# q, k and v of groups 1 to 14 as 49 products of 128 cubed, and a running count that places the other work around them

## The chip, the cores and the metric

One core of a Trainium2 chip runs the kernel. The metric is device time in microseconds (us), the median of several executions. The engines named below: TensorE (PE in the profile; its weight loads are the row PEld), VectorE (DVE), ScalarE (ACT), GpSimd (POOL), and the DMA queues that SyncE (SP) and GpSimd issue into. SBUF is the on-chip memory, PSUM the eight accumulation banks that TensorE writes.

## The reference

x holds 128 graphs of 64 nodes with 512 features, all in float32. Four layers follow one another, each of the form x = layernorm(x + f(x)):

```
layer 0:  y = relu(S (x W1) + b1), layernorm, S (y W2) + b2, plus x      (512 -> 1024 -> 512)
layer 1:  attention-like weights from y = x @ w, then A @ x @ w
layer 2:  x = relu(adj (x W1) + b1); x = relu(adj (x W2) + b2); adj (x W3) + b3
layer 3:  qkv = x @ Wqkv; 8 heads of 64; softmax over 64 nodes, mixed with adj and exp(-adj); times v; @ W_out + b_out
```

So each group of nodes passes through eleven products with 512x512 weights (W2 counts double), and between them small 64x64 products for each graph.

## The kernel before

**Tiling.** A group is 8 graphs, 512 rows, so there are 16 groups (NGRP) and every large product is 512x512x512. `multiply` (from L539 in the profile's rows on, through `product`) does it by Winograd's form of Strassen's scheme: four quadrants of 256, seven products of 256 cubed instead of eight. The seven are named B11, T1, T2, B21, T3, B22, T4. The left side's sums are made on DVE by `Left.sums` (L518 to L521), the sums on the weight's side are made once, by `Weight.making`, and kept in DRAM; `Weight.load` (L236, L238) brings one 256x256 tile for each product into a ring of RING = 20 tiles. `Stream.pump` issues these loads on SP's queue as ring slots come free. In a product, `ten.matmul` at L539 runs four times, each with a moving operand of 256 columns.

The results are joined as they come: the accumulators a and c are used again, their intermediate values go out by `snap` (u1, u5, u2: L555, on ACT, or on DVE where a residual or bias is added), and DVE adds the quadrants (L568 for the first, in bank b, which is "c_" in the names; L589; L598); the last is a copy on ACT (L608) or an add (L610).

**Stages.** Group q runs through `first_half` (a: layers 0 and 1) and `second_half` (b: layers 2 and 3); a step of the main loop works at the same time on group s in a, s-1 in b and s-2 in the tail t of `second_half` (the end of attention, Wout, the last layer norm). The lists `start`, `order`, `step_1`, `step_last` name the pieces in order, such as "b.q1", "b.k", "a.w1a"; a piece is what a generator does up to its next `yield`. Group 0 has its own path `first_group`, and group 15 ends in `last_rows`.

**Order.** Inside this, the framework's scheduler decides where an instruction goes on its engine, unless the code holds it: `in_turn` puts an instruction after the newest one of an engine, `behind(key)` after a recorded one, and engines in `strict` keep the order of the text. Each engine works through its own queue in order.

**Around the change.** In layer 3, `second_half` transposes x (L1186) into the left side xT, runs q, k, then `scores` (L1356, L1367), v, `softmax` (L1334 to L1342), `turn_probs` (L1391, L1398), `attend` (L1415), `taken` (L1430) and Wout. The tail's last `layer_norm` (bn_stats L457, sqrt L447, scaling L463) and its store stand between b.q and b.k. The scaling of layer 1's norm is split by `late`. bo is added to x by one DVE instruction (L1201), gb3 by four (L749, in `shifted`). `load` brings a group's x on SP's queue (`load_group`). Pools: ps_acc with 4 PSUM banks for the large products, pv and sps, ps_gt with 4 for the small ones; big with 8 tiles of 8 KB a partition.

Of the kernel before, what the change touches and what calls it, by code (L numbers as in the profile page):

```python
# [14 lines left out]
P = 128  # L15
C = 64
# [21 lines left out]
RING = 20  # L38
# [3 lines left out]
def kernel(  # L42
# [37 lines left out]
    big = ctx.enter_context(tc.tile_pool(name="big", bufs=8))  # L80
    sp = ctx.enter_context(tc.tile_pool(name="sp", bufs=3))
    work = ctx.enter_context(tc.tile_pool(name="work", bufs=7))
# [3 lines left out]
    ps_acc = ctx.enter_context(tc.tile_pool(name="ps_acc", bufs=4, space=bass.MemoryType.PSUM))  # L86
# [8 lines left out]
    nc.vector.memset(eps_t, EPS)  # L95

# [33 lines left out]

    ten, vec, act = Engine(nc.tensor, PE), Engine(nc.vector, DVE), Engine(nc.scalar, ACT)

    def load_group(q):
# [11 lines left out]
        else:  # L145
# [7 lines left out]
            nc.sync.dma_start(out=xg, in_=xsrc)  # L153
# [66 lines left out]
    class Weight:  # L220
        def __init__(self, src, col0, name, halves=1, scaled=False):
            self.src, self.col0, self.name, self.halves, self.scaled = src, col0, name, halves, scaled
            self.kept = []
# [5 lines left out]
        def tile(self, what, q, u):  # L229
            return wring.tile([P, 2, Q], FP, name=f"{self.name}{what}_{q}_{u}", tag="wq")  # L230

# [24 lines left out]
        def making(self, quads):  # L256
# [21 lines left out]
            with in_turn(POOL):  # L278
                for k, t in to_keep:
                    nc.gpsimd.dma_start(out=k, in_=t)  # L280
            yield got
# [46 lines left out]
    w_q, w_k, w_v = (Weight(Wqkv, n * D, f"w{'qkv'[n]}") for n in range(3))  # L328
# [5 lines left out]
    class Stream:  # L334


        def __init__(self, uses):
            self.todo = []
            for wt, q in uses:
                if q == 0:  # L340
# [10 lines left out]
        def pump(self, uses=None):  # L351
            end = len(self.todo) - uses if uses else 0
            while len(self.todo) > end and self.held + self.todo[0][3] <= RING:
                wt, q, what, n = self.todo.pop(0)
                self.held += n
                if what is None and q > 0:
# [42 lines left out]

        def done(self, wt, q, what):  # L400

            if q > 0:
                self.held -= wt.halves
            else:

                self.held -= 2 if what == ORDER[0] else 1
            self.pump()
# [43 lines left out]
    def layer_norm(xg, key, pairs=range(G), late=()):  # L451
# [7 lines left out]
        rs = rstd(mv, G, key, slice(pairs[0], pairs[-1] + 1))  # L459
# [7 lines left out]
        scale(p for p in pairs if p not in late)  # L467
        return lambda: scale(late)

# [34 lines left out]
    class Left:  # L504
# [9 lines left out]
        def sums(self):  # L514
# [3 lines left out]
            vec.tensor_add(s1, s3, self.quad(1, 1))  # L518
            vec.tensor_sub(s2, s1, self.quad(0, 0))
            vec.tensor_sub(s3, self.quad(0, 0), s3)  # L520
            vec.tensor_sub(s4, self.quad(0, 1), s2)  # L521
# [3 lines left out]
            }  # L525
            return self

    def product(acc, lefts, wt_q, what, first, last, flipped):
        ws = stream.take(*wt_q, what)
        n_k = 2 * len(lefts)  # L530
        for blk in range(2):
# [12 lines left out]
        stream.done(*wt_q, what)  # L544

    def multiply(lefts, wt_q, dst, key, flipped=False, res=None, stops=(3,), then=None, held={}, early=False):
# [6 lines left out]
        def snap(ps, m, n, what):  # L553
            t = work.tile([P, 2, Q], FP, name=f"{what}_{key}", tag="w")
# [5 lines left out]
        s1 = snap(pa, 0, 0, "u1")  # L560
# [3 lines left out]
        def first_quadrant():  # L564
            pb = ps_acc.tile([P, 2, Q], FP, name=f"c_{key}", tag="acc")
            product(pb, lefts, wt_q, B21, True, True, flipped)
            with behind(held.get(4)):
                vec.tensor_add(dst(0, 0), pb, s1)  # L568
            if then:
                then(0, 0, dst(0, 0))  # L570
# [17 lines left out]
        product(pa, lefts, wt_q, T3, False, False, flipped)  # L588
        last_add[f"{key}.d"] = vec.tensor_add(dst(1, 1), pa, s5).ins  # L589
# [6 lines left out]
        last_add[f"{key}.p6"] = newest(PE)  # L596
        with behind(held.get(6)):
# [9 lines left out]
        elif res is None:  # L607
            act.copy(dst(1, 0), pa)  # L608
        else:
            vec.tensor_add(dst(1, 0), pa, res(1, 0))  # L610
# [27 lines left out]
    def prepare(g):  # L638
# [49 lines left out]
        if q > 1:  # L688

            s_ps = [ps_acc.tile([P, G, C], FP, name=f"sps_{q}", tag="acc")] * 2  # L690
# [53 lines left out]

    def shifted(g, key):

        with behind(key):
            for p in range(G):
                vec.tensor_add(g["x"][:, p, :], g["x"][:, p, :], gb3_bc)  # L749
# [3 lines left out]
    def first_half(g):  # L753
# [6 lines left out]
        left.sums()  # L760
        yield "c1"
        h = [big.tile([P, 2, DH], FP, name=f"h_{q}_{m}", tag="big") for m in range(2)]
        for n in range(2):
# [8 lines left out]
            yield "w1" + "ab"[n]  # L772

# [837 lines left out]
```

## Time and profile before

| what | value |
|---|---|
| median of 3 runs | 2734.02 us (2733.93 to 2734.05) |
| the profiled execution, span | 2732.1 us |
| granted TensorE clock, mean | 1.000 |
| one group in the steady part (the same product of wo, 867.57 to 1035.54 us) | 167.97 us |
| DVE busy in it | 128.73 us |
| ACT busy in it | 49.36 us |
| DMA moved | 405.14 MB, 148 GB/s on average |
| a store of x, a load of x, a weight tile, from issue to landing | 5.2, 5.8, mostly 2.7 to 3.1 us |

The profiled execution is one run under the profiler; its span goes from the first to the last instruction, and the runs' median is 1.9 us longer. In a row of the groups, the columns are line, engine, operation, output<-inputs, shape and count; then the busy time, the mean of one in ns, and the idle time of the engine just before, with what ended it. In the order of time, a row begins with its start and its length, and merges equal neighbours. A row's length contains its tail, which overlaps with the next instruction: two DVE adds of 0.69 us follow each other at 0.60.

### The profile page before, as it was taken

The page shows a single profiled execution, that of the slowest core. Times are in us where ns is not written, and L with a number is a line of the kernel's source. Part 1 is how long each engine was busy: PE and PEld are TensorE (multiplying, and loading weights), DVE is VectorE, ACT ScalarE, POOL GpSimd, SP SyncE. Part 2 cuts the span into 40 slices and gives each one's busy share as a digit, 9 for nine tenths or more (in the row PEclk, how much of TensorE's full clock was granted, in tenths as well). Part 3 has the DMA queues.
Part 4 walks back from the last instruction along what each step waited for, and adds up shares of the span by engine and source line. Part 5 has one row for each costly group of instructions (what it writes and reads, how often), then busy time and mean ns, then how long its engine had stood idle before and what let it go on. Part 6 is the DMA issues. An engine that isn't in the chain of part 4 may idle for free.

```text
span 2732.1 us, 67726 instructions
## 1 busy us (share of the span) xinstructions
PE 2714.7 (99%) x28770; PEld 2347.7 (86%) x28770; DVE 2077.8 (76%) x4111; ACT 803.9 (29%) x1440; POOL 38.0 (1%) x71
## 2 busy tenths in 40 slices
PE   9999999999999999999999999999999999999998
PEld 7888888888888888888888888888888888888887
DVE  6878687876877778777786877778677687776766
ACT  3323223232232332323223233232322323233232
POOL 2000000000000000000000000000000000000000
PEclk9999999999999999999999999999999999999999
DMA  7545454454544545455454554545545455454541
GB/s 257 179 129 154 123 175 140 142 162 131 173 131 139 168 129 170 130 145 168 134 165 129 146 165 133 164 129 151 163 130 167 130 154 157 128 166 129 158 125 63
DMA packets 309532, 405.14 MB, mean 148 GB/s; under 512 B 57424, under 2 KB 185456, under 8 KB 309232
## 3 DMA queue, kind: packets, MB, share of 16 engines
q1 hardware_dynamic: 304256, 385.45, 48.2%
q0 software_dynamic: 4832, 15.24, 1.5%
q8 instruction: 228, 3.74, 0.6%
q14 instruction: 72, 0.59, 0.1%
q10 hardware_dynamic: 144, 0.13, 0.0%
HBM read 369.78 MB, written 30.93 MB: 147 GB/s over the span
## 4 chain that ended last, share of the span: by engine, by line
PE 96%; DVE 3%; ACT 1%; issue 0%; DMA 0%; DVEq 0%
PE a_l0w L539 15%; PE b_l0w L539 7%; PE a_l2b L539 4%; PE a_q L539 4%; PE a_k L539 4%; PE a_l2a L539 4%; PE a_v L539 4%; PE c_l0w L539 4%; PE a_l1w L539 4%; PE a_wo L539 4%; PE a_l2c L539 4%; PE gt_l L481 3%; PE gt_l0h L481 2%; PE b_l2a L539 2%; PE b_l1w L539 2%; PE b_l2b L539 2%
## 5 line engine op out<-in xcount | busy, mean ns | idle before, releaser
L539 PE MATMUL a_l0w<-w2w,aT_l0h 128*128 128x256 f32 x720 | 164.3, 381 | 0.0
L457 DVE BATCH_NORM_STATS2 st_l<-x 128x6 f32<-128x512 f32 x244 | 157.9, 676 | 0.6
L539 PEld LDWEIGHTS a_l0w<-w2w,aT_l0h 128*128 128x128 f32 x720 | 135.6, 190 | 18.8
L463 DVE TENSOR_SCALAR x<-x,mv_l,rs_l 128x512 f32<-128x512 f32 x244 | 119.3, 543 | 2.2
L539 PE MATMUL b_l0w<-w2w,s_l0h 128*128 128x256 f32 x480 | 108.5, 379 | 0.0
L783 ACT ACTIVATE h<-h 128x1024 f32<-128x1024 f32 (+1 forms) x58 | 55.0, 948 | 178.5 <-DVE h L598 157.4
L539 PEld LDWEIGHTS b_l0w<-w2w,s_l0h 128*128 128x128 f32 x480 | 91.1, 190 | 12.5
L1140 ACT ACTIVATE aT_h<-gth,gb_col 128x256 f32<-128x256 f32 x124 | 47.2, 491 | 159.0 <-PE gth L1128 159.0
L447 ACT ACTIVATE rs_l<-mv_l,eps_t 128x4 f32<-128x4 f32 (+1 forms) x63 | 18.8, 298 | 252.3 <-DVE mv_l L458 245.0
L492 ACT COPY aT_l<-gt_l 128x512 f32<-128x512 f32 x148 | 78.1, 597 | 46.4 <-PE gt_l L481 46.4
L555 DVE TENSOR_TENSOR u_l0w<-a_l0w,b_bc 128x512 f32<-128x512 f32 x56 | 38.6, 689 | 69.2 <-PE a_l0w L539 69.2
L539 PE MATMUL a_l2b<-gwbw,aT_h 128*128 128x256 f32 x360 | 86.6, 383 | 0.0
L539 PE MATMUL a_l2c<-gwcw,aT_h 128*128 128x256 f32 x360 | 86.3, 382 | 0.0
L539 PE MATMUL a_q<-aT_xT,wqw 128*128 128x256 f32 x360 | 85.1, 379 | 0.5 <-ACT aT_xT L1194 0.5
L539 PE MATMUL a_l1w<-ww,aT_l 128*128 128x256 f32 x360 | 85.1, 379 | 0.2 <-ACT aT_l L492 0.2
L539 PE MATMUL a_l2a<-aT_l,gwaw 128*128 128x256 f32 x360 | 85.0, 379 | 0.0
L539 PE MATMUL a_k<-aT_xT,wkw 128*128 128x256 f32 x360 | 85.0, 379 | 0.0
L539 PE MATMUL a_v<-wvw,aT_xT 128*128 128x256 f32 x336 | 81.1, 384 | 0.5 <-issue 0.5
L539 PE MATMUL a_l0w<-w1aw,aT_l 128*128 128x256 f32 x336 | 80.8, 383 | 0.0
L539 PE MATMUL a_wo<-wow,aT_oT 128*128 128x256 f32 x336 | 79.5, 379 | 0.0
L539 PE MATMUL a_l0w<-w1bw,aT_l 128*128 128x256 f32 x336 | 79.4, 379 | 0.0
L539 PEld LDWEIGHTS a_l2c<-gwcw,aT_h 128*128 128x128 f32 x360 | 67.2, 190 | 11.6 <-ACT u_l2c L555 3.0
(532 smaller groups left out, 6489.0 us busy)
## 6 DMA issues: line engine op xcount, KB each, us to landing
w2w<-w2k SPq DMA_DIRECT2D x210, 256.0 KB, 2.7
x<-in_x_dram SPq DMA_DIRECT2D x15, 1024.0 KB, 5.8
w1aw<-w1ak SPq DMA_DIRECT2D x60, 256.0 KB, 2.7
w1bw<-w1bk SPq DMA_DIRECT2D x60, 256.0 KB, 2.8
ww<-wk SPq DMA_DIRECT2D x60, 256.0 KB, 2.7
gwaw<-gwak SPq DMA_DIRECT2D x60, 256.0 KB, 3.4
gwbw<-gwbk SPq DMA_DIRECT2D x60, 256.0 KB, 2.7
gwcw<-gwck SPq DMA_DIRECT2D x60, 256.0 KB, 2.7
```

The lines of the kernel that those rows point to most:

```text
L447: act.activation(rs[:, at], mv[:, at, 1], AF.Sqrt, bias=eps_t)
L457: vec.bn_stats(st, xg[:, p, :])
L463: vec.tensor_scalar(xg[:, p, :], xg[:, p, :], mv[:, p, 0:1], rs[:, p : p + 1], ALU.subtract, ALU.mult)
L481: ten.matmul(ps[g][f * C : (f + 1) * C, c, p, :], src(2 * duo + p)[rows, c0 : c0 + C], mat[rows, 2 * duo + p, :], start=True, stop=True,)
L492: act.copy(o[:, :, :, g, :], ps[g])
L539: ten.matmul(acc[:, blk, :], lhsT, rhs, start=(first and blk == 0 and i == 0), stop=(last and i == n_k - 1), skip_group_check=True,)
L555: last_add[f"{key}.{what}"] = (act.copy(t, ps) if res is None else vec.tensor_add(t, ps, res(m, n))).ins
L783: act.activation(hn, hn, AF.Relu)
L1140: act.activation(o[:, :, h, :], cols, AF.Relu, bias=gb2_col[:, k : k + 1])
```

## The change

- q, k and v of groups 1 to 14 take Strassen's step twice. The class `Deep` lays the seven operands of the outer step in two halves of four and three (DEEP), makes the inner sums on DVE (`more_sums`), and `deep_multiply` runs the inner step's seven stages on both halves, for three weights one after the other and interleaved (`deep_stages`): 49 matmuls of 128x128x128 a weight. Stages end in copies on ACT or adds on DVE; `cross` and `outer_sums` join them. Groups 0 and 15 keep `multiply`.
- The weights' sums of the second step are made on POOL once (`make_deep`) and kept in DRAM; `load_deep` loads four or three 128x128 blocks in one DMA.
- From q to the end of the second W1 block (a.w1b), PE, DVE and ACT keep the order of the text, and an object `side` keeps a count of each engine's time. Other work (the layer 1 output and norm, the layer 3 norm, sums of left sides, relu and stats of h, doubling of x, softmax) is handed to it as generators that name the engine and the duration of each instruction, and it puts one where by its count the engine would else be idle.
- In every `multiply`, u1 is written into a PSUM bank of its own (ps_sum), on which B21 accumulates; the first quadrant is then copied by ACT. A first matmul "full" writes that bank once. ps_acc has 3 banks, and pv and sps use ps_gt.
- Layer norms of layers 1 and 3 scale on ACT (`norm_steps`); softmax takes the maximum negated, and eight exponentials of 64 columns on ACT with bias and sum.
- gb3 (groups 1 to 14) and bo are added to x by an accumulating DMA of POOL (`add_rows`), bo's behind a small copy that waits for the first result of `turn_probs`.
- x of groups 2 and up is loaded on POOL's queue after k (loadx), not with the rest of its group. RING is 16, big has 9 tiles, work 8. The order lists are rearranged around v, W1a and soft2.

```diff
-RING = 20
+RING = 16
+
+DEEP = ((B11, B21, T1, T2), (T3, T4, B22))
+STAGES = (B11, B21, B22, T1, T2, T3, T4)
+
+def deep_stages(n):
+
+    order = [(0, s) for s in (B11, T1, B21, T2, B22)]
+    for i in range(n):
+        if i + 1 < n:
+            order += [(i + 1, B11), (i, T3), (i + 1, T1), (i + 1, B21), (i, T4), (i + 1, T2), (i + 1, B22)]
+        else:
+            order += [(i, T3), (i, T4)]
+    return order
...
+    full = ps_sum.tile([P, T], FP, name="full", tag="sum")
+    nc.tensor.matmul(full, ones, ones[:, 0:1].to_broadcast([P, T]), start=True, stop=True)
...
+    class Side:
+        LATE, TOL, SEM = 0.27, 0.1, 0.12
...
+        def step(self, task):
+            e, us = task[1][:2]
+            self.clock[e] = max(self.clock[e], task[2]) + us
+            self.last = e
+            task[2] = self.clock[e] + self.SEM
+            task[1] = next(task[0], None)
...
+        def fill(self, limit):
+            while True:
+                found = None
+                for task in self.tasks:
+                    if task[1]:
+                        e, us = task[1][:2]
+                        at = max(self.clock[e], task[2])
+                        if at + us <= limit + self.TOL:
...
+        def run(self, us):
+            self.pe += us
+            self.fill(self.pe + self.LATE)
+
+        def spend(self, e, us):
+            self.clock[e] = max(self.clock[e], self.pe + self.LATE) + us
...
-            nc.sync.dma_start(out=xg, in_=xsrc)
+            g["load_x"] = lambda: (nc.gpsimd if q > 1 else nc.sync).dma_start(out=xg, in_=xsrc)
...
+        def make_deep(self, got):
+
+            self.deep_kept = []
+            for h, rs in enumerate(DEEP):
+                n = len(rs)
+                k = dram.tile([P, 7, n, P], FP, name=f"{self.name}deep{h}", tag=f"{self.name}deep{h}")
+                d = big.tile([P, 4, n, P], FP, name=f"{self.name}deep_{h}", tag="big")
+                for i, r in enumerate(rs):
+                    b = got[r][0].rearrange("p k (n c) -> p k n c", n=2)
+                    nc.gpsimd.tensor_sub(d[:, 0, i], b[:, 0, 1], b[:, 0, 0])
...
+                    nc.gpsimd.dma_start(out=k[:, 0:2, i], in_=b[:, :, 0])
+                    nc.gpsimd.dma_start(out=k[:, 2, i], in_=b[:, 1, 1])
+                nc.gpsimd.dma_start(out=k[:, 3:7], in_=d)
...
+    def norm_steps(xg, key, then=None, held=None):
...
+        for p in range(G):
+            yield "A", 0.55, p == 0
+            act.activation(
+                xg[:, p, :], xg[:, p, :], AF.Identity, bias=shift[:, p : p + 1], scale=rs[:, p : p + 1]
+            )
...
+        def outer_sums(j, h):
+            wt, dst, key, flipped = jobs[j]
+            r = {what: temps[j, h][:, i] for i, what in enumerate(DEEP[h])}
+            if h == 0:
+                yield "D", 0.6, 1
+                dst = dst()
+                vec.tensor_add(dst(0, 0), r[B11], r[B21])
...
+        def cross(j, h, at, to):
+            yield "D", 0.14 * len(DEEP[h]) + 0.07, 1
+            vec.tensor_add(to, snaps.pop((at, "u3")), snaps.pop((at, "u5")))
+
+        for at, s in deep_stages(2 * len(jobs)):
+            j, h = divmod(at, 2)
...
+            bank = "a" if s in (B11, T2, T3, T4) else "b" if s == B21 else "c"
+            fresh, last = s in (B11, T1), s in (B21, B22, T4)
+            if fresh:
+                banks[at, bank] = ps_acc.tile([P, 4, P], FP, name=f"{bank}{h}_{key}", tag="acc")
...
+                ten.matmul(ps[:, i], lhsT, rhs, start=fresh and i == 0, stop=last, skip_group_check=True)
+            stream.done(wt, q, (h, s))
+            side.run(0.2233 * n)
...
+            if s == B22:
+                vec.tensor_add(sub(0, 1), ps, snaps.pop((at, "u2")))
+                side.spend("D", 0.07 + 0.134 * n)
+            else:
+                side.spend("A", 0.05 + 0.109 * n)
+                if s == B11:
+                    banks[at, "b"] = ps_sum.tile([P, 4, P], FP, name=f"b{h}_{key}", tag="sum")
+                    act.copy(banks[at, "b"][:, :n], ps)
...
-        s1 = snap(pa, 0, 0, "u1")
+        pb = snap(pa, 0, 0, "u1", ps_sum.tile([P, 2, Q], FP, name=f"c_{key}", tag="sum"))
...
-            pb = ps_acc.tile([P, 2, Q], FP, name=f"c_{key}", tag="acc")
-            product(pb, lefts, wt_q, B21, True, True, flipped)
-            with behind(held.get(4)):
-                vec.tensor_add(dst(0, 0), pb, s1)
+            product(pb, lefts, wt_q, B21, False, True, flipped)
...
+                act.copy(dst(0, 0), pb)
...
+    def add_rows(xg, row):
+
+        nc.gpsimd.dma_start(out=xg, in_=row.unsqueeze(1).to_broadcast([P, G, D]), accum_op=ALU.add)
...
+            side.start(1.5)
...
+            more = side.add(left.more_sums(), 0)
+            for _ in range(4):
+                side.step(more)
...
         pts = [turn_probs(g, duo, probs[duo]) for duo in range(2)]
+        if 0 < q:
+            due = small.tile([P, 1], FP, name=f"due_{q}", tag="due")
+            with in_turn(POOL):
+                nc.gpsimd.tensor_copy(due, pts[0][0][:, 0, 0:1])
+            with in_turn(POOL):
+                add_rows(xg, bo_bc)
...
+        for n in range(8):
+            yield "A", 0.34, n == 0
+            act.activation(d[:, n], d[:, n], AF.Exp, bias=mx[:, n : n + 1], accum_out=sm[:, n : n + 1])
...
-        t.v1 a.c1 t.v b.gt t.soft a.w1a1 a.w1a t.soft2 a.resid b.l2a1 b.l2a a.w1b1 t.ptp a.w1b t.pv a.lnh b.l2b1
+        t.v1 t.v2 a.c1 t.v a.w1a1 b.gt t.soft a.w1a a.resid b.l2a1 b.l2a a.w1b1 t.soft2 t.ptp a.w1b t.pv a.lnh b.l2b1
...
-        rows3 a.p1 b.xT a.p2 b.q1 a.ln1 b.q t.ln3 b.k1 b.k prep b.dots
+        rows3 a.p1 b.xT t.ln3 a.p2 b.q1 a.ln1 b.q b.k1 b.k loadx b.v0 prep b.dots
```

## The prediction

> **What bounds the kernel now.** I read the page's busy shares first, then the chain of waits, then the order of TensorE's work in one steady group, then the other engines over the same stretch.
>
> ```profile
> span 2732.1 us, 67726 instructions
> PE 2714.7 (99%) x28770; PEld 2347.7 (86%) x28770; DVE 2077.8 (76%) x4111; ACT 803.9 (29%) x1440; POOL 38.0 (1%) x71
> ...
> PE 96%; DVE 3%; ACT 1%; issue 0%; DMA 0%; DVEq 0%
> ```
>
> TensorE has work in nearly the whole span and 96% of the chain runs through it. So time leaves only if TensorE's own stream gets shorter, and any wait that reaches it is paid in full. All terms below are against this execution (span 2732.1 us; the median of the runs, 2734.02, is 1.9 us more).
>
> ```profile
> 898.37 1.89 PE L539 MATMUL a_q<-aT_xT,wqw 128*128 128x256 f32 x8
> 900.10 1.89 PE L539 MATMUL a_k<-aT_xT,wkw 128*128 128x256 f32 x8
> ...
> 927.44 1.89 PE L539 MATMUL a_v<-wvw,aT_xT 128*128 128x256 f32 x8
> 929.26 2.10 PE L481 MATMUL gt_l<-atc,x 64*64 64x64 f32 x128
> 931.29 1.99 PE L539 MATMUL a_l0w<-w1aw,aT_l 128*128 128x256 f32 x8
> 933.12 1.89 PE L539 MATMUL b_l0w<-w1aw,s_l 128*128 128x256 f32 x8
> ```
>
> Columns: start, length, engine, line, tiles, shape, count. One 256-cubed product is 4 matmuls, and each float32 matmul is recorded as two instructions, so 8. Products start 1.73 us apart (from 888.01 to 910.46, the last product of k, are 13 steps of 1.727): 0.216 us an instruction, 12.09 us a weight. The product that follows a block of small matmuls takes 1.99 instead of 1.89: its first weight load could not be hidden, 0.10 us.
>
> **The change, part by part.**
>
> **49 small products.** A weight becomes 7x7 products of 128 cubed: 49 matmuls, 98 instructions with a moving operand of 128 columns, in place of 56 of 256. No row of before has 128 columns. By columns alone an instruction is 0.108; the nearest rows on both sides say more. In the 64x64 block at 929.26, four quadrants work side by side, 32 instructions each; from the first start to the last (2.10 less the row's mean of 0.22) are 1.88 us, 31 steps of 0.0606. Between 0.0606 at 64 columns and 0.216 at 256 the straight line gives 0.0606 + 0.155/3 = 0.112 at 128. Below: 0.108. Above: the load not hidden at all, 0.108 + 0.104 = 0.212. I take 0.112, since the 64x64 block too loads as many columns as it streams, one load for each matmul, and still keeps to 0.0606. Then a weight takes 98 x 0.1124 = 11.01 us, 1.08 less, and 3 weights x 14 groups give **-45 us** (-63 at 0.108, +365 at 0.212).
>
> The Trainium skill, "TensorE: Matmul & The Clock Gate", section "Back-to-back issue gap", speaks against this: in a real stream of load and matmul pairs it gives about 81 ns at 128 columns where the matmul alone would allow 56, since the loads set the pace. That ratio would make the instruction some 0.157 us (an estimate from that page), a weight 15.4, and the whole +139 us. The trace disagrees at 64 columns, as said, and the sum goes by the trace.
>
> **More sums.** DVE and ACT prices, by rows of the same stretch:
>
> ```profile
> 887.18 0.68 DVE L598 TENSOR_TENSOR y<-b_l1w,u_l1w 128x512 f32<-128x512 f32 x1
> 887.78 0.68 DVE L519 TENSOR_TENSOR s_xT<-s_xT,aT_xT 128x512 f32<-128x512 f32 x1
> 888.38 0.69 DVE L520 TENSOR_TENSOR aT_xT<-aT_xT 128x512 f32<-128x512 f32 x1
> ...
> 884.48 2.05 ACT L1194 COPY aT_xT<-xtp 128x512 f32<-128x512 f32 x4 [3.37 <-PE xtp L1186]
> ```
>
> A DVE add of 512 columns costs 0.60 in a row (start to start), of 384 some 0.47 (256 columns last 0.43, 512 last 0.69); an ACT copy 0.49, of 384 columns 0.38. Per weight DVE now does 3 adds (1.8). After: two B22 adds, two cross adds, seven outer adds, 1.07 + 1.1 + 4.2 = 6.4, so +13.8 for q, k, v; the inner sums of the left side add 4 x (0.61 + 0.47) = +4.3. Taken off DVE in a group: the first quadrant's add in 8 other multiplies (-4.8), the scaling of two layer norms (8 x 0.48, -3.8), bo and gb3 (-4.7), half of the softmax passes (8 x 0.6, -4.8). Net about 0 on 128.7 of 167.9 us. ACT gains 8 copies (+3.9), three times 5.2 less 2.0 (+9.6), 8 scalings (+4), and 32 exponentials of 64 columns near 0.34 for 4 of 0.6 (+8.5; between the row of 4 columns, 0.30, and of 256, 0.49): 49.4 becomes some 75 of 165. As totals nothing is short. What matters is the stretch where the new sums stand:
>
> ```profile
> 888.00:900.00 12.00, 12.00 (x57) 10.57 (x56) 11.60 (x24) 2.64 (x5) 0.00 (x0) 1.00 0.48 145
> 900.00:912.20 12.20, 12.20 (x58) 10.52 (x56) 8.44 (x17) 2.56 (x5) 0.00 (x0) 1.00 0.73 216
> 912.20:931.30 19.10, 19.10 (x458) 16.76 (x457) 14.88 (x26) 8.58 (x15) 0.00 (x0) 1.00 0.63 190
> ```
>
> Columns after the length: busy PE, PEld, DVE, ACT, POOL; clock, DMA share, GB/s. From q to the second small block DVE is busy 34.9 of 43.3 us. After, the stretch that ends at b.gt is 33.0 (products) + 2.4 (dots) + 2.1 (a.c1) + 5.2 (three W1a products) = 42.7. Its DVE work: 34.9 - 2.2 (bo) - 3.8 (scalings) - 7.5 (softmax, now later) + 18.1 + 1.8 (W1a's three u) = 41.3, of which the last outer sums of v, some 3, can wait until soft2: 38.3, or 90%. The first row shows that TensorE lost nothing where DVE was busy 11.60 of 12.00, so it can fit. But each product needs a bank back in 1.3 to 1.6 us, and a DVE instruction in the wrong place costs 0.6 at once. Cost per group: at best 0, at worst as in the rival below; I take 0.7, a little more than one misplaced add, **+10 us** for 14 groups.
>
> **First quadrant and banks.** In the other multiplies u1 goes into a PSUM bank of its own and B21 adds onto it, so B21 waits for that copy. Two products, 3.45 us, lie between, and the copy takes some 0.25 to start and 0.6 to run: 0; in group 0, where B21 comes second in one multiply, under 1 us once. pv and sps move to the four banks of the small blocks, whose copies (2.05 for four) end long before the next small block, 5 us or more later: 0.
>
> **Weights.** SP issues 42 loads a group instead of 21, at about 0.35 us each (the rows on its queue read 0.32 and 0.38) 14.7 of 33 us: 0. A quarter-size tile of 256 KB lasts 4 x 0.225 = 0.90 us, so the stage draws 291 GB/s where a product of 1.73 us draws 152. The DMA share reached 1.02 at 318 GB/s (912 to 915 us), so 9.63 MB a group take 30.1 of 33.0 us; with out and x (1 MB each, 3.3 us each) it is 36.7, and the 16 tiles held ahead (12.6 us of work) cover the 3.7 that are missing: **0**. If that cover were gone, the price is those 3.7 us a group.
>
> **x and the row adds.** The load of x goes from SP's queue, early in the step, to POOL's after k, behind the bo and gb3 adds. It waits for the store of the group three before: 5.2 + 0.54 + 5.8 = 11.5 us by their rows, while from loadx to a.c1 lie 34 small matmuls and the dots, 7.6 + 2.4 = 10.0. The store is released in the q stage if the running count finds ACT free, some 20 us earlier; then it costs **0**, else 1.5 a group. An accumulating DMA has no row here: between a plain 1 MB load, 5.8, and three times that, 17, for reading twice and writing. gb3 has some 30 us until agg reads x, bo some 60 until wo: **0**. The new wait on POOL is the copy "due", which waits for the first pt of turn_probs; behind it stand the bo add, the next gb3 add and the next load of x, and the first of these is wanted some 60 us later.
>
> **Once.** make_deep gives POOL 28 subtractions and 16 DMAs a weight (0.54 each, a 128-column operation 0.2 to 0.3): some 16 us on top of 2.2, while its ring slots stay taken, and the ring has 16 instead of 20. v's 8 slots come free only when q's are read. Between 0 and 16 us; I take **+5**, since q's POOL work mostly lies beside the 12 us of q. The matmul "full" runs while TensorE waits for its first data: 0.
>
> **Sum:** 2732.1 - 45 + 10 + 5 = 2702 for the execution, 2704 with the 1.9; with the rounded terms I name 2702.
>
> **Rivals.**
> DVE becomes the bound (slower). Its order is now fixed by a count; if it keeps the idle share of before in this stretch (34.9 of 43.3, 81% busy), 38.3 us of work take 47.5, 4.8 more than TensorE has: 67 us lost in 14 groups against 45 won, 2732 - 45 + 67 + 5 = **2759**. Against it stands the 97% of the row above; for it, that every add waits for a product just ended. It decides from 3.2 us a group (45/14).
> x comes late at a.c1: +1.5 a group or a little more with the weights on the same engines, **2723**. For it: 909 to 918 us ran at a DMA share of 0.92 to 1.02 even before. Against: the store should leave early.
> Loads not hidden at 128 columns: **3097**. Against: the 64x64 block.
> Stalls just eat the gain: **2734**. It takes 3.2 us a group, and nothing points to just that.
>
> **How the numbers follow.** Forecast 0.68 (its own range 2686 to 2722: 63 saved and 17 lost, or 45 saved and 35 lost), x late 0.08, DVE bound 0.15, loads 0.03, no change 0.06. Below 0.2% (5.5 us) the runs tell nothing. Faster 0.68 + 0.08 = 0.76, same 0.06, slower 0.18. From 2686 to 2742 lie nearly all of the first two, no change, and the near end of the DVE case: about 0.82.
>
> **What would show it.** Rows of 128x128 matmuls near 0.112 us start to start, q, k and v in 33 us a group plus a small remainder; TensorE's idle time before those rows put down to DVE or ACT if the sums are late, to DMA if weights or x are; POOL busy some 50 us more before 300 us. Wrong: a step above 0.115 (42 x 98 x 0.003 = 12 us), idle time above 3.2 us a group, or a first group several us longer than now.

## The result and the profile after

The changed kernel takes 2749.85 us (median of 4 runs, 2744.72 to 2751.85), the kernel before 2733.97 beside it: a ratio of 1.0055, 95% interval [1.0041, 1.0070]. It is slower by 16 us, where 32 us less were forecast. The profiled execution (2744.72 us, span 2742.9) is the fastest of the four; the others ran at a granted clock of 0.995 against its 0.996. It is 10.8 us longer than the execution of before, and the accounts below are made against that.

The page of the changed kernel:

```profile
span 2742.9 us, 74095 instructions
PE 2691.6 (98%) x30536; PEld 2377.5 (87%) x30536; DVE 2092.4 (76%) x4169; ACT 1231.5 (45%) x2860; POOL 162.6 (6%) x259
...
q1 hardware_dynamic: 323072, 428.59, 50.2%
q0 software_dynamic: 25968, 68.92, 10.6%
q8 instruction: 243, 3.98, 0.6%
...
PE 91%; DVE 5%; ACT 2%; issue 1%; POOL 1%; DMA 0%; DVEq 0%; ACTq 0%; POOLq 0%
```

TensorE works 23 us less than before (2714.7), so its stream did get shorter, and yet the span is longer: TensorE waits. The three middle lines are DMA queues (packets, MB, share of the 16 engines). GpSimd's queue q0 moves 69 MB where it moved 15. Queue q8 matters below. Its 3.98 MB over TensorE's 61072 instructions (30536 matmuls and as many weight loads) are 65 bytes each, and in the kernel before 3.74 MB over 57540 are 65 as well. So it is TensorE's program, which comes in during the run, in packets of 16 KB, over the same 16 engines.

What the change was for is there. In the order of time, in group 4:

```profile
906.02 1.73 PE L145 MATMUL a_q<-d_xT,wqd 128*128 128x128 f32 x14
```

Fourteen instructions in 1.73 us, each 0.275 long with its tail: (1.73 - 0.275) / 13 = 0.112 us from start to start. A group that nothing disturbs is shorter too: the first product of gW1 (layer 2's first weight, once in every group) starts, before and after, at

```profile
1111.45 1.89 PE L539 MATMUL a_l2a<-aT_l,gwaw 128*128 128x256 f32 x8
1279.42 1.89 PE L539 MATMUL a_l2a<-aT_l,gwaw 128*128 128x256 f32 x8
```

```profile
1123.37 1.89 PE L145 MATMUL a_l2a<-aT_l,gwaw 128*128 128x256 f32 x8
1288.85 1.89 PE L145 MATMUL a_l2a<-aT_l,gwaw 128*128 128x256 f32 x8
```

167.97 us before, 165.48 after: 2.5 us saved, 35 in 14 groups. By the starts of TensorE's instructions in this stretch, q, k and v take 33.5 us instead of 36.8, 3.2 less (45 in 14 groups); 0.7 comes back in layer 1's products of w and in the transposes of x just ahead of q. Two losses eat what is saved.

**A loss once.** The same product of group 1 starts at 269.69 before and at 284.85 after. Between 243 and 252 us of the changed kernel:

```profile
244.27 0.47 POOL L338 TENSOR_TENSOR wkdeep<-wkt,wkdeep 128x128 f32<-128x128 f32 x1
245.11 0.69 DVE L379 TENSOR_TENSOR wvt<-wvb,wvb 128x512 f32<-128x512 f32 x1 [2.68 <-DMA wkdeep<-wkt]
...
249.20 0.90 DVE L380 TENSOR_TENSOR wvt<-wvb,wvt 128x512 f32<-128x512 f32 x1 [3.39 <-DMA wkdeep<-wkt]
250.36 0.67 DVE L914 TENSOR_TENSOR kT<-a_k,u_k 128x512 f32<-128x512 f32 x1
251.09 1.22 PE L860 MATMUL a_k<-d_xT,wkt 128*128 128x256 f32 x2 [4.21 <-DVE kT L914]
```

VectorE is to write a sum of w_v's tiles into a ring slot that still holds a tile of w_k, and make_deep's store of that tile (DMA wkdeep<-wkt, on GpSimd's queue) has not ended. It waits 2.68 and 3.39 us, and since it works in order, the add of kT stands behind it and TensorE waits for that add. The granted clock adds to the loss:

```profile
200.00:220.00 20.00, 17.79 (x207) 14.26 (x198) 15.97 (x27) 8.00 (x14) 19.89 (x36) 0.91 0.58 198
240.00:260.00 20.00, 15.79 (x192) 12.76 (x192) 9.16 (x16) 2.49 (x5) 18.81 (x39) 0.83 0.71 251
```

The columns behind the length are busy PE, PEld, DVE, ACT and POOL, then clock, DMA share and GB/s. A mean of 0.91 and of 0.83 in 20 us are 3.4 and 6.8 us at half clock, which can cost up to 5 of the 15 us; before has none there.

**A loss again and again.** TensorE's waits, by what ended them (total us, times, longest):

```profile
PE a_v L145 <- issue: 7.0, 3, 2.6
PE dot L145 <- issue: 6.9, 5, 2.3
PE gt_l L145 <- issue: 5.5, 5, 1.9
PE a_k L860 <- DVE kT L914: 4.2, 1, 4.2
```

"issue" means that the instruction waited for nothing that the profile shows. Two of these stops in order of time, and the same stretch in windows (columns as above):

```profile
430.91 0.83 PE L145 MATMUL a_v<-wvd,d_xT 128*128 128x128 f32 x6
434.05 0.38 PE L145 MATMUL a_v<-wvd,d_xT 128*128 128x128 f32 x2 [2.31 <-issue]
...
436.53 1.84 PE L145 MATMUL gt_l<-smat,x 64*64 64x64 f32 x107
440.25 0.57 PE L145 MATMUL gt_l<-smat,x 64*64 64x64 f32 x21 [1.88 <-issue]
```

```profile
428.00:430.00 2.00, 2.00 (x140) 2.00 (x136) 1.16 (x4) 0.30 (x1) 0.00 (x0) 1.00 1.07 368
430.00:434.00 4.00, 1.74 (x26) 1.59 (x17) 2.42 (x5) 0.48 (x1) 0.00 (x0) 1.00 1.03 358
```

Both stops fall in the middle of a block, between instructions of the same kind, the first at a DMA share of 1.03. I counted them in the trace: gaps above 0.6 us from start to start of TensorE's instructions (weight loads included), between 400 and 2690 us, that end within 3.2 us of the start of a packet of the instruction queue. Before has 2, of 2.5 us in all; after has 16, of 28.4 us. In all of them the next matmul starts 1.2 to 1.6 us after the packet has landed. The profile puts 2 of the 16 down to ACT instead of "issue"; one of these (a_l2b, 2.4 us) falls in the middle of a product, and five of the runs below stop at the same place with "issue".

The account of the profiled execution: 14 groups x -2.45 (2.5 in thirteen, 1.7 in the last, by groups without a stop) = -34, +15 once, +26 in stops, +3.8 that remain, together +10.8. Of the 3.8, up to 3.4 are two stretches of half clock, one after each of two long stops. The windows around them have a mean clock of 0.83, that is 3.4 us of ten at half clock, which cost up to 1.7 each:

```profile
1770.00:1780.00 10.00, 7.66 (x175) 7.28 (x174) 4.56 (x9) 2.59 (x6) 0.00 (x0) 0.83 0.75 263
2110.00:2120.00 10.00, 8.21 (x163) 7.73 (x163) 3.62 (x7) 3.87 (x8) 0.00 (x0) 0.83 0.50 167
```

### The profile page after: what moved, and what is told of

Read it like the earlier page. It is cut to its first block, busy times and chain, and to the rows that moved or that the text cites. A ratio compares the mean times of both kernels' runs of the same rounds, so it can differ in the third digit from the quotient of the medians.

```text
span 2742.9 us, 74095 instructions
## 1 busy us (share of the span) xinstructions
PE 2691.6 (98%) x30536; PEld 2377.5 (87%) x30536; DVE 2092.4 (76%) x4169; ACT 1231.5 (45%) x2860; POOL 162.6 (6%) x259
## 3 DMA queue, kind: packets, MB, share of 16 engines
q0 software_dynamic: 25968, 68.92, 10.6%
q8 instruction: 243, 3.98, 0.6%
## 4 chain that ended last, share of the span: by engine, by line
PE 91%; DVE 5%; ACT 2%; issue 1%; POOL 1%; DMA 0%; DVEq 0%; ACTq 0%; POOLq 0%
PE a_l0w L860 8%; PE a_l0w L145 7%; PE a_l2b L860 4%; PE a_l2c L860 4%; PE b_l0w L860 4%; PE a_wo L860 4%; PE a_v L145 4%; PE b_l0w L145 3%; PE a_l2a L145 3%; PE a_k L145 3%; PE a_q L145 3%; PE a_l1w L860 3%; PE gt_l0h L632 2%; PE gt_l L145 2%; PE c_l0w L860 2%; PE b_l2c L860 2%
## 5 line engine op out<-in xcount | busy, mean ns | idle before, releaser
L145 ACT ACTIVATE sm<-sm,mx 128x64 f32<-128x64 f32 x416 | 139.1, 340 | 0.2
L145 PE MATMUL a_v<-wvd,d_xT 128*128 128x128 f32 x700 | 95.4, 280 | 9.1 <-issue 7.0
L145 PEld LDWEIGHTS a_v<-wvd,d_xT 128*128 128x128 f32 x700 | 85.9, 193 | 11.2 <-issue 7.1
L145 PE MATMUL a_k<-d_xT,wkd 128*128 128x128 f32 x700 | 91.9, 275 | 0.0
L145 PE MATMUL a_q<-d_xT,wqd 128*128 128x128 f32 x700 | 91.9, 275 | 0.0
L145 ACT ACTIVATE x<-x,shift_l,rs_l 128x512 f32<-128x512 f32 x112 | 91.7, 819 | 0.0
L145 PEld LDWEIGHTS a_q<-d_xT,wqd 128*128 128x128 f32 x700 | 85.9, 192 | 0.7
L145 PEld LDWEIGHTS a_k<-d_xT,wkd 128*128 128x128 f32 x700 | 84.9, 192 | 0.0
L583 DVE BATCH_NORM_STATS2 st_l<-x 128x6 f32<-128x512 f32 x128 | 82.4, 676 | 1.6
L145 ACT ACTIVATION_READ_ACCUMULATOR sm<-sm,mx 128x1 f32 x416 | 80.2, 193 | 0.0
```

The costliest lines, as they stand in the source:

```text
L145: return op(*args, **kwargs)
L583: vec.bn_stats(st, xg[:, p, :])
```

## The experiments

Theory: the steady loss is TensorE's own program arriving late, because the transfers that the change adds fill the engines; the loss once is the price of make_deep. Rivals: the stops come of the denser instruction stream alone; the early loss comes of the shorter ring.

**The loss once: e5_nomake, e3_deferred, e10_owntile.** The first takes the making away:

```diff
-                k = dram.tile([P, 7, n, P], FP, name=f"{self.name}deep{h}", tag=f"{self.name}deep{h}")
...
+                src = x[at : at + rows, :].rearrange("r d -> (r d)")
+                self.deep_kept.append(src.rearrange("(p s r c) -> p s r c", s=7, r=n, c=P))
```

> The changed kernel without the one-time making of the 128-column weight tiles: no GpSimd differences and none of their stores; the tiles are loaded, in the same sizes and at the same places, from memory of the input x, so q, k and v of groups 1 to 14 are not the reference's. Theory one (the early 15 us are the price of the differences on GpSimd, which hold tiles of the ring and slow VectorE): the lag of the first product of gW1 in group 1 behind the kernel before falls from 15.2 us to under 5, and the time to 2733 to 2740; the stops without a shown reason stay at some 16 and 28 us. Rival (the early loss comes of the shorter ring, 16 tiles instead of 20): the lag stays above 10 us and the time above 2743.

2736.43 us, 1.0004 of before [0.9995, 1.0014], 13.4 less than the changed kernel; the product of group 1 starts at 271.73, a lag of 2.0 behind the kernel before instead of 15.2, with the same ring, and the clock is whole up to 400 us. The stops are unchanged, 17 of 27.4 us. The rival (ring) falls: make_deep costs 13 us, the half clock at its waits included, and the changed kernel without it only equals the one before.

e3_deferred moves the making into step 2, and reads the blocks back into tiles of the pool `big`:

```diff
-                if self.deep:
-                    self.make_deep(got)
...
+                    t = big.tile([P, 2, 8, P], FP, name=f"{self.name}deep_{h}{i0}", tag="big")
...
+    for name, after in (("deepq", "t.v"), ("deepk", "b.l2a"), ("deepv", "t.ptp")):
+        step_2.insert(step_2.index(after) + 1, name)
```

> The changed kernel, but make_deep reads its blocks again from DRAM in the second step instead of from ring slots in the first. Theory for the one-time loss (14.9 us more than before at the first xtp of group 1; POOL is busy 90 us in the first step, keeps ring slots, and DVE waits 6 us for them): that offset falls to 3 to 6 us, the time by 9 to 12 us, to 2733 to 2742. Rival (the smaller ring alone does it): the offset stays at 12 to 15 and the time too.

The lag at group 1 fell to 2.8 us as expected, but the time is 2772.34, 1.0141 [1.0126, 1.0156]. TensorE's waits in it:

```profile
PE a_l2b L863 <- DVE g L917: 14.4, 1, 14.4
PE gt_l0h L635 <- ACT aT_oT L1898: 13.6, 1, 13.6
```

```profile
323.72 2.06 ACT L1898 ACTIVATE aT_oT<-pv 128x512 f32<-128x512 f32 x4 [17.51 <-DMA wkdeep<-wkdeep]
```

ScalarE's copy into aT_oT, a tile of the same pool, waited 17.5 us for a slot that the making held, and everything in order behind it. The loss moved some 60 us later with the slots, and grew. So e10_owntile gives the making two small tiles of its own:

```diff
+    mkp = ctx.enter_context(tc.tile_pool(name="mkp", bufs=2))
...
+                t = mkp.tile([P, 4, P], FP, name=f"{self.name}mk{h}{i}", tag="mk")
...
+                    (nc.gpsimd.tensor_sub, (b00, b01, b00)),
+                    (nc.gpsimd.tensor_sub, (b01, b11, b01)),
+                    (nc.gpsimd.tensor_sub, (b11, b11, b00)),
+                    (nc.gpsimd.tensor_sub, (b10, b10, b11)),
```

> The changed kernel with the 128-column tiles made in step 2 instead of in step 1: GpSimd reads each of the 21 blocks back from memory into two small tiles of its own, makes the four differences in place and stores them; nothing of the ring or of the big tiles is held. Theory (the one-time loss comes of held tiles and of VectorE slowed down in the first steps): the lag of the first gW1 product of group 1 falls from 15.2 to under 5 us, some of it comes back in step 2 (84 differences beside VectorE), 2735 to 2742. Rival (the differences cost the same wherever they stand): 2746 to 2753.

A miss: 2745.54, 1.0044 [1.0029, 1.0059], lag 14.1. In its trace GpSimd was already making the differences at 224 us, in step 1 after all, and the stores of w_k's sums, on the same queue, went out only at 243. VectorE waited for those before it could overwrite the slots, and half clock adds up to 7 us to the lag (from 93 and from 246 us, 6.8 us each; e12 below has a shorter such stretch at 93 us without any making):

```profile
DVE wvt L397 <- DMA wkk<-wkt: 6.9, 1, 6.9
```

In e11_both below the differences run in the same stretch beside VectorE (GpSimd at 221 to 240 us), but fewer tiles are held and the slots are free: there the lag is 2.6, with whole clock. So the time goes with the slots held, not with VectorE slowed by GpSimd.

**The stops: e1_shared, e12_light.** The same instructions of TensorE, fewer bytes. e1 loads the 128-column tiles for the first half of each weight only:

```diff
-                        self.todo += [(trio[i // 2], q, (i % 2, s), 1) for i, s in deep_stages(6)]
+                        self.todo += [(trio[i // 2], q, (i % 2, s), 1) for i, s in deep_stages(6) if i % 2 == 0]
...
-            return self.here.pop((wt, q, (h, s)))
+            return self.here[wt, q, (0, s)] if h == 0 else self.here.pop((wt, q, (0, s)))
```

> The changed kernel, but the quarter-size weight tiles are loaded only for the first half of each weight; the second half's matmuls read the same tiles, so outer products T3, T4 and B22 of q, k and v use the weights of B11, B21 and T1, and the outputs of groups 1 to 14 are not the reference's. TensorE's instructions, their order and their number stay; a group loads 5.5 MB of these tiles instead of 9.6. In the changed kernel 17 stops inside blocks of matmuls, 30 us in all between 400 and 2700 us, end 1.2 to 1.6 us after a 16 KB instruction fetch lands, and those fetches start late where the DMA share is near 1. Theory (full DMA engines hold up TensorE's instruction fetch): the DMA share in the last 25 us of the stage falls from 1.0 to below 0.8, these stops sum to under 8 us, and the time falls by 22 to 32 us, to some 2715 to 2727. Rival (more instructions per us outrun the fetch, whatever the DMAs do): the stops stay at 25 to 35 us and the time within 5 us of the changed kernel's 2744 to 2752. Second rival (DVE and ACT are late, the stops are theirs): no change either.

2728.65, 0.9979 of before [0.9970, 0.9988]: 21 us less than the changed kernel, with the lag at group 1 still 17.2. The stops are 9, of 11.9 us: fewer, but not under 8 us. Whether the rest needs the transfers too, e12 asks: no making, and seven tiles a group for all six halves.

```diff
-                        trio = (w_q, w_k, w_v)
-                        self.todo += [(trio[i // 2], q, (i % 2, s), 1) for i, s in deep_stages(6)]
+                        self.todo += [(w_q, q, (0, s), 1) for i, s in deep_stages(6) if i == 0]
...
+            return self.here[w_q, q, (0, s)][:, : len(DEEP[h])]
```

> The changed kernel without the making of the tiles (they come from x, as before) and with one set of seven tiles loaded a group for q, k and v, 1.8 MB instead of 9.6, used for all six halves; q, k and v of groups 1 to 14 are not the reference's. TensorE's instructions, their order and their density are those of the changed kernel. Theory (a late fetch needs both, transfer engines near full and dense instructions): the stops without a shown reason fall from 28 us to under 4, and the time to 2700 to 2714. Rival (density alone makes 10 us or more of stops): 2716 to 2728.

2714.30, 0.9927 [0.9912, 0.9942], at the edge of the time that the theory named and just outside the rival's. The stops are 9, of 11.2 us, where the theory had under 4 and the rival 10 or more. Those at the scores are gone; those in the next small block stay:

```profile
PE gt_l L145 <- issue: 4.8, 4, 1.7
PE a_v L145 <- issue: 1.5, 1, 1.5
```

So 17 of the 28 us need the added bytes, and some 11 stay without them, although e12 moves less than the kernel before (383 MB against 405), which has 2.5 us of stops. Even those mostly fall at busy engines. I sorted every packet of the instruction queue between 400 and 2690 us by the DMA share around it (3 us before its start to 1 us after) and by how many instructions, weight loads included, TensorE started in the 6 us before:

```
packets (stops)   share under 0.6,          share 0.6 or more,
                  under 150   150 or more   under 150   150 or more
before             48 (0)      102 (0)       23 (0)      20 (2)
after              43 (1)       78 (0)       40 (2)      47 (13)
e1_shared          52 (1)       95 (2)       35 (0)      27 (6)
e12_light          64 (1)       92 (1)       19 (0)      33 (7)
e8_busydma2        38 (0)       95 (0)       33 (0)      18 (6)
```

Under a share of 0.6 a packet was late 1 time in 100 (6 of 707), also behind dense instructions (3 of 462); from 0.6 on, behind dense instructions, 1 time in 4 (34 of 145). By this count it takes both. The dense stretches are not the 49 products alone: a matmul and a load each 0.112 us are 107 in 6 us, and it takes a block of 64x64 products (256 instructions in 2.1 us) to bring 150. Both kernels have as many of these, 122 packets before and 125 after. What the change moves is the share around them, at the scores and small blocks that stand beside and behind q, k and v: 20 packets with 0.6 or more before, 47 after, 33 in e12. What else the 11 us of e12 need stays open.

**The stops in the old stream: e4_busydma, e8_busydma2.** The other way round: the kernel before, with copies of x to unused memory behind the k products.

```diff
+            due = small.tile([P, 1], FP, name=f"due_{q}", tag="due")
+            with in_turn(POOL):
+                nc.gpsimd.tensor_copy(due, kT[:, 0, 0:1])
+            for n in range(3):
+                spare = dram.tile([T, D], FP, name=f"spare{n}_{q}", tag=f"spare{n}")
+                with in_turn(POOL):
+                    nc.gpsimd.dma_start(out=spare, in_=x[q * T : (q + 1) * T, :])
```

e4 has the same lines without `in_turn`.

> The kernel before, with three plain 1 MB copies from DRAM to DRAM of each group 1 to 14, issued by POOL when the first quadrant of kT is written; nothing reads them. They fill the DMA engines for some 10 us around dots, v and the two small blocks, where TensorE's instruction stream is the old one. Full-DMA theory: stops that end 1.2 to 1.6 us after an instruction fetch lands, in before 2 of them (2.4 us), become 6 to 14, and the time rises by 6 to 25 us. Density rival: 0 to 2 stops more, time within 3 us of before.

2839.05, and it tells nothing: the scheduler put all the copies into the first 200 us, where the DMA share is 0.95 and TensorE busy for 98 us of 200. In e8 they stand where they were meant to.

> The kernel before, with three copies of 1 MB from x to unused memory in each of the groups 1 to 14, issued on GpSimd's queue in order behind the k products, and not computed with. The instruction stream of TensorE stays the old one. Theory (full transfer engines make instructions late, in any stream): stops without a shown reason rise from 2 to 6 or more, and the time by 6 to 25 us, 2740 to 2760. Rival (the stops come of the changed stream, 128 columns an instruction, and not of the transfers): 2 or 3 stops, 2731 to 2738.

2865.36, far above the range, for a reason that I had not counted: 79.8 us are waits for x, whose load was caught behind the copies, and the granted clock is 0.981 in the mean. But the stops are the test, and they rose from 2 to 6, of 20.3 us, in a stream of 256-column products that had nearly none:

```profile
586.42 1.35 PE L539 MATMUL a_v<-wvw,aT_xT 128*128 128x256 f32 x5
591.84 1.65 PE L539 MATMUL a_v<-wvw,aT_xT 128*128 128x256 f32 x3 [4.07 <-issue]
```

```profile
585.00:590.00 5.00, 2.77 (x107) 2.22 (x98) 4.47 (x9) 0.00 (x0) 0.00 (x0) 0.99 1.16 395
590.00:595.00 5.00, 3.16 (x8) 2.53 (x9) 0.49 (x1) 1.40 (x2) 0.00 (x0) 0.50 0.47 131
```

A product of eight stops after its fifth instruction, with the engines at 1.16. A packet of the instruction queue landed at 590.5, and the sixth instruction started at 591.84; the clock was then half for 5 us. So full transfer engines make the program late without the changed stream; all six stops fall in the v products and the small block behind them.

**The row adds: e2_poolrows, e6_dverows.** gb3 and bo added by GpSimd, or by VectorE as before, instead of by accumulating transfers (during one, from 1285 to 1292 us of the changed kernel, the DMA share is 1.05 at only 220 GB/s):

```diff
-        nc.gpsimd.dma_start(out=xg, in_=row.unsqueeze(1).to_broadcast([P, G, D]), accum_op=ALU.add)
+        nc.gpsimd.tensor_add(xg, xg, row.unsqueeze(1).to_broadcast([P, G, D]))
```

> The changed kernel, but gb3 and bo are added to x by one POOL instruction each in place of an accumulating DMA. Full-DMA theory: of the stops, the one behind the bo add (2.5 us, once) goes, those at the end of v stay, since the adds run later in the step; DVE may lose some 0.2 us an instruction while POOL works. Time 2738 to 2750. If the accumulating DMAs held up x or the weights generally, the time would fall by more than 10 us.

A miss: 2824.27, 1.0335 [1.0320, 1.0350], and still 13 stops.

```profile
457.11 4.80 POOL L1075 TENSOR_TENSOR x<-x,gb_bc 128x2048 f32<-128x2048 f32 x1 [31.19 <-ACT aT_l L145]
...
458.10 4.36 DVE L145 TENSOR_TENSOR s_l<-aT_l 128x512 f32<-128x512 f32 x1
...
464.90 1.56 PE L145 MATMUL a_l0w<-w1aw,aT_l 128*128 128x256 f32 x3 [2.63 <-DVE h L145]
```

The VectorE add that usually takes 0.68 us takes 4.36: it ends at 462.46 after GpSimd's ends at 461.91. The Trainium skill says this in "SBUF — State Buffer", section "SBUF: two separate sides": GpSimd and a VectorE operation with two inputs from SBUF want the same ports, the first takes them for its whole instruction and "the other fully blocks". The row agrees. With the adds on VectorE instead:

```diff
+        for p in range(G):
+            vec.tensor_add(xg[:, p, :], xg[:, p, :], row)
```

> The changed kernel with the gb3 and bout rows added by VectorE, four additions of 128x512 at each place, instead of by the two accumulating transfers. Theory (full transfer engines make TensorE's instructions late): the stops that fall behind the two accumulating transfers go, 4 to 10 us, and VectorE, idle a quarter of the time, takes 5.5 us more a group: 2738 to 2747. Rival (VectorE is in order, and eight additions in front of snapshots and quadrant additions make TensorE wait some 1 to 2 us a group): 2755 to 2775.

2759.86, 1.0096 [1.0081, 1.0111], in the rival's range. The stops fell only from 28.4 to 25.1 us, and an undisturbed group lost some 0.65 us around the first gW2 products. Which of the moved instructions costs that stays open. In both cases the accumulating transfers are the better choice.

**Fewer bytes at once: e7_early, e9_paced.** e7 ends the last norm early and moves store and load of x ahead of q:

```diff
-        for _ in range(G + 2):
-            next(steps)
-        g["ln3"] = steps
+        whole(steps)
...
-rows3 a.p1 b.xT t.ln3 a.p2 b.q1 a.ln1 b.q b.k1 b.k loadx b.v0 prep b.dots
+rows3 a.p1 b.xT t.ln3 loadx a.p2 b.q1 a.ln1 b.q b.k1 b.k b.v0 prep b.dots
```

> The changed kernel with the last layer norm of the group before ended, and its output stored, as soon as its sums are there, and the load of the next x issued right behind it, ahead of the q products instead of behind the k products. The same bytes, but 2 MB less beside the 9.6 MB of the 128-column tiles in the 25 us in which the transfer engines are full. Theory (full engines make instructions late): the stops fall by a third to a half, 2732 to 2742. Rival one (the 2 MB only start the full stretch sooner, the sum of bytes between the xT turn and the scores is the same): within 4 us of the changed kernel, 2746 to 2754. Rival two (3.3 us of ScalarE in one piece ahead of the snapshots cost TensorE 1 to 3 us a group): above 2758.

2788.10, 1.0198 [1.0183, 1.0213]; rival two. The stops stay at 28.8 us, and the four scalings, 2.93 us in one piece on ScalarE, stand ahead of the first copy of q in every group:

```profile
PE b_q L145 <- ACT b_q L145: 30.1, 14, 2.2
```

This also prices the running count: with the scalings spread by it, that wait is not there. e9 limits how far the other weights are loaded ahead:

```diff
+            def room():
+                wt, q, what, n = self.todo[0]
+                plain = 1 < q < NGRP - 1 and not wt.deep
+                return self.held + n <= (9 if plain else RING)
```

> The changed kernel with one limit altered: a weight tile other than the 128-column ones of q, k and v is loaded ahead only while no more than 9 tiles are held, instead of 16. The same bytes; the refill for the weights that follow q, k and v no longer falls into the stretch in which the transfer engines are full. Theory (full engines make TensorE's instructions late): the stops without a shown reason fall from some 28 us to under 14, and the time to 2731 to 2741. Rival one (it is the denser instruction stream alone): the stops stay and the time is within 4 us of the changed kernel. Rival two (9 tiles ahead, some 15 us, are too few, and products wait for their weights): waits of TensorE for weight transfers, above 2755.

2742.92, 1.0039 [1.0026, 1.0051], 7 us less than the changed kernel, between the theory and its rival. The stops fell only to 24.4 us: the full stretch starts some 7 us earlier (0.92 instead of 0.69 at 1235 to 1245 us) and ends earlier, and is hardly shorter, for the bytes are the same. Most of the gain is elsewhere: the lag at group 1 is 6.4 us (9.1 where x is turned into xT, where the changed kernel has 14.9), and no half clock stands there. Fewer tiles are held in the ring when make_deep runs, which is the likely reason.

**Together: e11_both, e13_paced5.** Own tiles and the limit of 9; then the making held behind work of step 2, and a limit of 5.

> Both edits: tiles made in step 2 with GpSimd's own small tiles, and no more than 9 tiles held ahead of the other weights. If both terms of the theory hold they add: 2717 to 2730, below the kernel before. If either fails, its rival's price shows in the same way as alone, and the time lies above 2733.

2737.79, 1.0013 [1.0004, 1.0023], above the range: the lag is 2.6, but the stops are 27.3 us, so the second term of the theory fails.

```diff
+            with behind(dict(q="l0w10_2", k="l2a_1", v="l0w11_2")[who[4]]):
+                dict(q=w_q, k=w_k, v=w_v)[who[4]].make_deep()
```

> The tiles made in step 2, held back behind work of that step so that the stores of the k and v tiles go first, and no more than 5 tiles held ahead of the other weights, so that the 128-column tiles are loaded earlier and nothing is refilled beside the scores. Theory: the first gW1 product of group 1 lags by under 4 us, the stops fall under 20 us, 2717 to 2733. Rival (5 tiles, some 9 us, are too few beside landings of 3 to 7 us): waits of TensorE for weights, above 2740.

2736.00, 1.0009 [1.0000, 1.0019], above the range: the lag is 2.1, the stops are still 24.4 us, and there is no wait for weights. It is the best that computes all of the reference, and equals the kernel before. None was found that beats it; the 9.6 MB a group would have to become fewer, as in e1 and e12, which leave part of the loading out.

## Why the prediction was wrong

- **49 small products, -45 us: right.** 0.112 us an instruction was predicted and is measured. The figure of the Trainium skill that spoke against it ("TensorE: Matmul & The Clock Gate", "Back-to-back issue gap") would have made it 0.157 by the prediction's estimate; in this stream of pairs 128 columns keep to 0.112, loads included. In an undisturbed group q, k and v take 3.2 us less, 45 in 14 groups.
- **More sums, +10 us: right in size.** An undisturbed group saves 2.5 us, the -45 and +10 together predict 35/14 = 2.5. But the 0.7 us that come back stand in the products of w and the transposes ahead of q, not at a misplaced add in the stretch of the new sums, so the size is partly luck. VectorE's total came as worked out (76%), and the rival in which it becomes the bound did not happen. ScalarE is 45% busy instead of 29%.
- **Weights, 0: the step that failed.** That the 16 tiles held ahead "cover the 3.7 that are missing" asked only whether the weights come in time, and they do: no wait of TensorE for a weight transfer shows. Not asked was what else comes through the engines once they are full: the program. It has no issue row and no semaphore, so no rival contained it. Measured: 26 us more of stops, 17 of which go when the bytes go (e12), and up to 3.4 us of half clock behind them; what the other 9 need besides a busy engine is not shown. "Stalls just eat the gain" was given 0.06, because nothing pointed to 3.2 us a group. Something pointed to its kind, if not its size: a wait of 1.3 us in the kernel before, at a DMA share of 1.01 (1920.4 to 1924.4 us), which I had not followed:

```profile
PE b_v L539 <- issue: 1.3, 1, 1.3
```

- **Once, +5 us: mis-sized.** It measured 13 (e5). I counted GpSimd's operations at 0.2 to 0.3 us, and alone they take 0.45, up to 1.06 in the mean of a group of rows beside VectorE; and I laid them beside q's 12 us, where they run from 200 to 280 us. The path was named ("its ring slots stay taken"), its price was not worked out: VectorE in order behind a slot, kT behind that, TensorE behind kT, and half clock around it.
- **x and the row adds, 0: right.** No wait for x shows after the change; where it is late by force, in e8, it costs up to 8 us a group. That the row adds fill the engines (q0 10.6% instead of 1.5%) belongs to the failed step, but with them on VectorE (e6) only 3 of the 28 us of stops go.
- **First quadrant and banks, 0: right**; no such wait appears.

Without both losses the forecast would have been nearer: e12_light, with neither the making nor most of the bytes, takes 2714, 11 of it in the stops that it keeps. The forecast without its +5 for the making is 2697 for the execution, 2699 for the median.

## What to carry to other kernels

When a change adds transfers beside TensorE's work, work out the DMA share of each stretch, and treat a share near 1 with dense small matmuls as a risk to TensorE itself, also where every tile comes in time: in the page of before, look for waits put down to "issue" in the middle of a block. Price one-time work not by the engine that does it but by the buffers that it holds and by what stands in order behind them. A wait that shows once or twice in the old profile is the place where a heavier load will show many times.

## What the runs showed of the hardware

- TensorE's instructions arrive during the run in packets of 16 KB over the shared transfer engines. A late one stops TensorE by 0.6 to 4.5 us, mostly with no releaser in the profile. After two stops of 2.4 and 2.6 us the clock was half for 3.4 us (after others of 2.6 and 2.8 it was not), and after one of 4.5 us in e8 for 6.8.
- A GpSimd addition of 128x2048 takes 4.8 us and blocks a VectorE addition with two SBUF inputs for its whole length (4.36 instead of 0.68 us).
- On ScalarE an exponential with a sum output is followed by a read of the accumulator: 0.34 us and 0.19 us for 64 columns, where the running count allows 0.34 for both.
